# A two-layer relational graph convolution: a third pass of summing tiles from x, and the order of its steps

## The chip, the cores and the metric

The kernel runs on one core of one Trainium2 chip. The core has five engines that run side by side and meet at semaphores: PE (TensorE, matrix products into PSUM), DVE (VectorE), ACT (ScalarE), POOL (GpSimd) and SP (SyncE). Here POOL issues the indirect gathers, and SP and ACT issue all other DMAs. The metric is the time of one execution on the device in microseconds (us), as the median of several runs.

## The reference

There are 12500 nodes with 128 features each and 200000 edges, sorted by destination, each with one of eight types. A layer takes, for each node and each type, the mean over the node's edges of this type of the source's features times the type's matrix, adds up the types, adds the node's own features times a root matrix and a bias, and ends with a relu and a residual:

```python
W = jnp.einsum('rb,bio->rio', comp, basis)
xw = jnp.einsum('ni,rio->nro', x, W)
msgs = xw[src, et]
seg = dst * N_REL + et
summed = jax.ops.segment_sum(msgs, seg, num_segments=N_NODES * N_REL)
cnt = jax.ops.segment_sum(jnp.ones((msgs.shape[0],), x.dtype), seg, num_segments=N_NODES * N_REL)
mean = summed / jnp.maximum(cnt, 1.0)[:, None]
agg = mean.reshape(N_NODES, N_REL, HIDDEN).sum(axis=1)
return agg + x @ root + bias
...
for l in range(N_LAYERS):
    h_new = _rgcn_conv(h, src, dst, edge_type, basis[l], comp[l], root[l], bias[l])
    h_new = jax.nn.relu(h_new)
    h = h_new + h
...
x = _layernorm(x + _L0_gnn_ref(x, edge_index, edge_type_8, ...), axis=-1)
```

Only the sources are in no order, so each edge's source row has to be fetched from memory.

## The kernel before

**Tiles and octets.** The edges are cut into 1563 tiles of 128 edges, and eight tiles make an octet; there are 196 octets (the last one is short). Both layers go through the octets in order. In code and text, layer 1 is `l == 0` and layer 2 is `l == 1`. Layer 1 gathers rows of x, takes means by type and only then multiplies by the types' matrices. For layer 2 the finished features are multiplied by all eight matrices ahead of time, into a table `y_d` in memory with one row for each node and type, and layer 2 gathers rows of that table.

**Where a tile's rows come from.** Nearly all tiles get theirs from one indirect DMA each, issued by POOL (`gather`, line 814), into a ring of seven octet buffers (`rows_r`). The gather of octet o + 5 is issued in octet o, into the buffer that octet o - 2 used, so that it waits for PE's means of octet o - 2. The last six octets of a layer are gathered two octets ahead, and behind PE's latest means. 56 tiles of layer 1 are read row by row from SP's and ACT's queues (`lone_rows`, line 750). Eight more, two groups of four (`JOINED`, tiles 1112 to 1115 and 1504 to 1507), are not gathered but *summed from x*.

**Summing four tiles from x** (`joining`). A pass runs through all of x in 98 blocks of nodes. For each block DVE makes a one-hot matrix of 512 edges against the nodes (line 1516), and PE multiplies the block of x with it and adds the product up in the PSUM bank `ct` (line 1531). After 98 blocks each of the 512 edges' columns has its source row; DVE copies the sum out, PE transposes it in four parts, and DVE copies the rows into the buffer `joined`, where PE's means find them as they would find gathered rows. x comes in 13 loads of up to 512 KB over ACT's queue into two buffers (`xb`), and the one-hots have four buffers (`eqb`). `JOINED` gives for each pass its first tile, its first octet and its last: 84 to 132 and 135 to 183, that is two blocks in an octet. `join(o, 0)` issues the loads of octet o, `join(o, 1)` DVE's part, and `join(o, 2)` PE's products for the one-hots made in octet o - 1. The buffers lie in the arena where the destinations and types of the edges stood, so that the checks that read these have to be done before.

**The order in an octet of layer 1** (the loop `for o in range(NG - 3)`). Each engine runs its own instructions in this order: the gather (POOL); the means, 8 products of gathered rows with one-hots of edges (PE, line 1340); `batch`: copies of table halves, of the product before and of the means out of PSUM (ACT); `join(o, 0)`; the single rows; edge preparation; the one-hots for the means of octet o + 2 (DVE, line 1240); `join(o, 1)`; some steps of the checks (`run(later, ...)`); the finishing of nodes; the product of octet o - 1 with the matrices (PE, line 1372); `join(o, 2)`; the placing of octet o - 2 (PE, line 1403); and one or two halves of the table's tiles from octet 50 on (PE, line 1558, with a copy by ACT or DVE), two as long as more than six wait and in the last 16 octets. The class `Plan` turns this one list into waits: an instruction waits for the writer and the readers of what it touches that stand *ahead of it in the list*.

**The checks.** A generator (`checks`) gives 124 steps: the second layer's matrices, 13 times 7 steps on edges, 11 on spans, 9 on places, 11 of a fix list for the first 16 tiles of layer 2 (`fix_list`, PE lines 1167 and 1188), and a last one. It starts in octet 43, when the edges are prepared, with three steps an octet up to octet 83 and one from 84 on.

**The turn of the layers.** The first two octets of layer 2 are gathered from the part of the table that belongs to the first 94 node tiles; octet 2 begins with one gather of the fix list (line 808) and waits for the whole table.

Of the kernel before, what the change touches and what calls it, by code (L numbers as in the profile page):

```python
# [428 lines left out]
def ordered_path(  # L429
# [26 lines left out]
    P = 128  # L456
# [11 lines left out]
    Q = 8  # L468
# [20 lines left out]
    SOON = 16  # L489
    DONE = NT - 4  # L490
    LONG = 9
    JOINED = [(1112, 84, 132), (1504, 135, 183)]
    SUMMED = {52: (3, 45), 98: (49, 91), 144: (95, 137), 190: (141, 183)}
    assert D == P and R * K == P and B == BF + 1 and 1 < TL and LAST < P and BF % 4 == 0 and Q == G and N % 2 == 0
    main = slice(HALO, HALO + P)
# [5 lines left out]
    def keep(shape, dtype, name):  # L501
        return const.tile(shape, dtype, name=name)
# [71 lines left out]
    def part_of(n, *cell):  # L574
        nonlocal free_at
        free_at += n
        assert free_at <= at
        used_c.append(cell)
        return arena[:, free_at - n:free_at], cell

    M = 4
    xb_b = [part_of(S * D, "xb", i) for i in range(2)]
    eqb_b = [part_of(M * P, "eqb", i) for i in range(4)]
    ends_b = part_of(M * P, "ends")
    joined_b = [part_of(M * P, "joined", i) for i in range(len(JOINED))]
    joined = {t + i: (joined_b[k][0][:, i * P:(i + 1) * P], [joined_b[k][1]])
              for k, (t, _, _) in enumerate(JOINED) for i in range(M)}
    room_c += used_c
    p_8 = keep([P, S + 2], F32, "p_8")
# [2 lines left out]
    first = keep([P, B], F32, "first")  # L592
# [53 lines left out]
    def vec(emit, reads=(), writes=()):  # L646
        plan.add("DVE", emit, reads, writes)
# [4 lines left out]
    def pe(emit, reads=(), writes=()):  # L652
        plan.add("PE", emit, reads, writes)
# [4 lines left out]
    def load(out_t, in_t, reads=(), writes=(), q="SP"):  # L658
        e = nc.sync if q == "SP" else nc.scalar
        plan.add(q, lambda: e.dma_start(out_t, in_t), reads, writes, lane="hw" if q == "SP" else "aq")  # L660
# [7 lines left out]
    def in_turn(emits):  # L668
        def emit():
            for e in emits:  # L670
                last = e()
            return last

        return emit
# [592 lines left out]
    def shape_of(n):  # L1267
        m = min(GN, N - n * GN)
        return (P, S) if m == GN else (m // 2, 2)

    def in_rows(a, n):
        p, k = shape_of(n)
        return a[n * GN:n * GN + p * k, :].rearrange("(p s) d -> p (s d)", s=k)
# [201 lines left out]
    def joining(k):  # L1475

        tile0, first, end = JOINED[k]
        n = end - first + 1
        slots = [(g, i) for g in range(NX) for i in range(shape_of(g)[1])]
        assert len(slots) == NT  # L1480
        takes = {q: [] for q in range(first - 1, end + 3)}
        for j in range(NT):
            takes[first + j * n // NT].append(j)
        used = {g: [q for q, js in takes.items() if any(slots[j][0] == g for j in js)] for g in range(NX)}
        loads = {}
        for g in range(NX):
            loads.setdefault(max(first - 4 + g, JOINED[k - 1][2] + 2 if k else 0) if g < 2 else used[g - 2][-1] + 2, []).append(g)
        (e_t, e_c), (f_t, f_c), (j_t, j_c) = ends_b, eqb_b[0], joined_b[k]
        f3, j3 = (t.rearrange("p (t c) -> p t c", t=M) for t in (f_t, j_t))
        b, bc = ct_b  # L1490
        done = end + 1
        assert max(len(v) for v in takes.values()) <= 2
        assert tile0 // Q >= done + 3 and (k == 0 or first >= JOINED[k - 1][2] + 3)

        def load_b(g):
            p, m = shape_of(g)
            t, c = xb_b[g % 2]
            load(t[:p, :m * D], in_rows(x, g), [], [c] + (free_c if k == 0 and g < 2 else []), "ACT")

        def start_of(q):  # L1500
            if q == first - 4:
                assert checked and parts is None
                load(j_t.bitcast(I32), bass.AP(tensor=src.tensor, offset=src.offset + tile0 * P,
                                               ap=[[0, P], [1, M * P]]), [], [j_c] + free_c, "ACT")
            for g in loads.get(q, ()):
                load_b(g)

        def before(q):
            if q == first - 2 and k == 0:
                x_nodes()  # L1510
            if q == first:
                vec(lambda: nc.vector.tensor_copy(e_t, j_t.bitcast(I32)), [j_c], [e_c] + (free_c if k == 0 else []))
            for j in takes.get(q, ()):
                p = shape_of(slots[j][0])[0]
                o, oc = eqb_b[j % 4]
                vec(lambda j=j, p=p, o=o: nc.vector.tensor_tensor(  # L1516
                    o[:p], e_t[:p], x_node[:p, j:j + 1].to_broadcast([p, M * P]), op=ALU.is_equal),
                    [e_c, "x_node"], [oc])
            if q == done + 1:
                vec(lambda: nc.vector.tensor_copy(f3, b), [bc], [f_c])  # L1520
            if q == done + 2:
                vec(lambda: nc.vector.tensor_copy(j3, b), [bc], [j_c])
            plan.mark("DVE")

        def after(q):
            for j in takes.get(q - 1, ()):
                g, i = slots[j]
                p, m = shape_of(g)
                t, c = xb_b[g % 2]
                o, oc = eqb_b[j % 4]  # L1530
                pe(lambda j=j, p=p, i=i, t=t, o=o: nc.tensor.matmul(  # L1531
                    b.rearrange("p t c -> p (t c)"), t[:p, i * D:(i + 1) * D], o[:p], start=j == 0, stop=j == NT - 1),
                    [c, oc], [bc])
            if q == done + 1:
                pe(in_turn([lambda i=i: nc.tensor.transpose(b[:, i, :], f3[:, i, :], ident) for i in range(M)]),
                   [f_c, "ident"], [bc])
            plan.mark("PE")

        return start_of, before, after

    joins = [joining(k) for k in range(len(JOINED))]

    def join(o, part):
        for (_, first, end), f in zip(JOINED, joins):
            if first - 4 <= o <= end + 3:
                f[part](o)
# [307 lines left out]
    def sup(q):  # L1854
        return (q * Q + G) // (2 * G) - 1
# [13 lines left out]
    def run(gen, n):  # L1869
        for _ in range(n):  # L1870
            if next(gen, gen) is gen:
                return True
        return False
# [39 lines left out]
    def checks():  # L1913
        weights(1, (pt_b, pt_b))
        yield
        for b in range(B):
            yield from check_edges(b)
        yield from check_span()
        yield from check_place()
        yield from fix_list()  # L1920
        yield check_all()

    later = checks()
# [32 lines left out]
    for o in range(NG - 3):  # L1956
        if o + CLOSE == NQ - 2:
            gather(0, NQ - 1)
        gathers(0, o)
        means(o)  # L1960
        batch(o)
        join(o, 0)
        if o == 1:
            where()
            load_offsets()
        if o > 1:
            lone_rows(0, "SP", o)
        for i in range(2 if o < FIRST else 1):
            if parts is not None and run(parts, 1):
                parts = None  # L1970
        onehot(0, o + 2, o - 1)
        join(o, 1)
        if parts is None:
            run(later, 3 if o < 84 else 1)
        if o > 1:
            lone_rows(0, "ACT", o)
        if not opened:
            end()
        for step in opened:
            step()  # L1980
        opened.clear()
        if o > 0:
            product(o - 1)
            if o < SOLO:
                take_product(o - 1)
            else:
                late_y.append(o - 1)
        for step in behind:
            pe(*step)
            plan.mark("PE")  # L1990
        behind.clear()
        join(o, 2)
        if o > 1:
            k = place(o - 2)
            close(k)
            if k is not None and k % S == S // 2 and k // S + 1 < NX:
                n = k // S + 1
                turned_to.extend([turn_x(n, h) for h in range(-(-shape_of(n)[1] // 4))])
                turned_to.append((lambda n=n: load_x(n + 1), None))
        for i in range(2):  # L2000
            if turned_to:
                a, b = turned_to.pop(0)
            elif tables and o >= TABLE and (i == 0 or len(tables) > 6 or o > NG - 16):
                a, b = tables.pop(0)
            else:
                break
            while copies:
                copies.pop(0)(vcopy)
            a()
            if b is not None:  # L2010
                copies.append(b)
# [69 lines left out]
    for q in range(NQ):  # L2081
# [4 lines left out]
        k = sup(q)  # L2086
# [116 lines left out]
```

## Time and profile before

| | |
|---|---|
| median of 3 runs | 3730.01 us (3728.68 to 3738.03) |
| the profiled execution | 3738.43 us |
| its span, first to last instruction | 3736.6 us |
| PE busy | 2986.0 us (80%) |
| DVE busy | 2354.0 us (63%) |
| ACT busy | 354.5 us (9%) |
| POOL busy | 2812.0 us (75%) |
| DMA, mean | 80 GB/s |
| granted PE clock, mean | 0.937 |

Times in the profile are microseconds from the first instruction. A row of a group reads: line, engine, operation, what it writes from what it reads, shapes, count, then busy time in us and the mean of one in ns, then the idle time of the engine just before these instructions and what ended most of it. "issue" is idle time that ends with nothing that the profile shows. A row of a timeline reads: start, length, engine, line, operation, operands, count, and in brackets the idle time before and what ended it. A row by stretches reads: stretch, its length, then busy time and count for each engine shown (PE, its weight loads, DVE, ACT, POOL in this order, or one engine alone), the granted PE clock, the share of the DMA engines' time, and GB/s.

### The profile page before, as it was taken

The numbers are of one execution on the slowest core, as the hardware profiler recorded it, in microseconds if no ns is written. First come the engines' busy times: TensorE is split into PE (matmuls) and PEld (weight loads), VectorE is DVE, ScalarE is ACT, GpSimd is POOL, SyncE is SP. The second block draws the span as 40 slices with busy tenths as digits, with TensorE's granted clock in tenths as the row PEclk, the third lists the DMA queues.
The fourth block names the chain that finished last, engine by engine and source line by source line (L and its number), as shares of the span: only waits on it lengthen the run. The fifth ranks groups of instructions, "written<-read, shape, count | busy, mean of one in ns | idle before, by whom it ended". The sixth has DMA issues, their size and how long they took to land.

```text
span 3736.6 us, 69352 instructions
## 1 busy us (share of the span) xinstructions
PE 2986.0 (80%) x13831; PEld 2137.2 (57%) x13831; DVE 2354.0 (63%) x5786; ACT 354.5 (9%) x795; POOL 2812.0 (75%) x2977
## 2 busy tenths in 40 slices
PE   5777757778877778877778888888888888798896
PEld 3666645565655556655555555555555555555554
DVE  5556435545554445445456778787777787787885
ACT  1121212111111111111100000000000000000000
POOL 7777777777777777777777777777777777777776
PEclk7999889989999999999989999999999999999998
DMA  4122123334333333332332222222222222222222
GB/s 126 55 62 61 56 89 106 117 115 123 112 101 100 91 104 106 95 106 92 99 97 56 55 56 67 67 62 67 56 73 62 62 67 62 67 66 56 68 66 61
DMA packets 159970, 299.91 MB, mean 80 GB/s; under 512 B 67108, under 2 KB 90358, under 8 KB 159534
## 3 DMA queue, kind: packets, MB, share of 16 engines
q0 software_dynamic: 95008, 194.77, 20.4%
q10 hardware_dynamic: 34755, 68.94, 5.7%
q1 hardware_dynamic: 29771, 31.73, 3.2%
q14 instruction: 325, 2.66, 0.2%
q8 instruction: 111, 1.82, 0.2%
HBM read 236.52 MB, written 58.65 MB: 79 GB/s over the span
## 4 chain that ended last, share of the span: by engine, by line
POOL 47%; issue 17%; PE 16%; DMA 9%; ACTq 4%; ACT 3%; DVE 2%; SPq 1%; POOLq 0%; DVEq 0%
POOL rows L814 47%; DMA rows<-y_d,idy 7%; PE y L1372 4%; ACTq L750 3%; PE s L1340 3%; PE s L1726 2%; PE pt L1558 1%; ACTq L745 1%; PE ct L1531 1%; ACT sT L663 1%; SPq L750 1%; ACT y_row L663 1%; DVE dm L1240 1%; PE ct L1010 1%; PE ct L1011 1%
## 5 line engine op out<-in xcount | busy, mean ns | idle before, releaser
L814 POOL DMA_INDIRECT rows<-in_x_dram,idx x1499 | 1420.0, 947 | 459.8 <-issue 451.1
L814 POOL DMA_INDIRECT rows<-y_d,idy x1469 | 1390.0, 946 | 449.8 <-issue 440.2
L1726 PE MATMUL s<-dm,rows 128*128 128x256 f32 x2932 | 777.2, 417 | 260.7 <-DMA rows<-y_d,idy 235.8
L1240 DVE TENSOR_SCALAR dm<-cols,near,w 128x256 f32<-128x256 f16 x1531 | 709.6, 537 | 386.1 <-PE s L1726 376.4
L1726 PEld LDWEIGHTS s<-dm,rows 128*128 128x128 f32 x2932 | 592.4, 210 | 376.4 <-DMA rows<-y_d,idy 233.7
L1240 DVE TENSOR_SCALAR dm<-cols,kr,w 128x128 f32<-128x128 f16 x1563 | 525.9, 403 | 137.4 <-PE s L1340 112.5
L1372 PE MATMUL y<-w_sb,sT 128*128 128x128 f32 x3136 | 443.8, 300 | 203.9 <-ACT ys L663 150.6
L1372 PEld LDWEIGHTS y<-w_sb,sT 128*128 128x128 f32 x3136 | 406.7, 209 | 240.3 <-ACT ys L663 177.6
L1340 PEld LDWEIGHTS s<-dm,rows 128*128 128x128 f32 x2998 | 382.2, 201 | 184.0 <-issue 159.1
L1340 PE MATMUL s<-dm,rows 128*128 128x128 f32 x2998 | 401.6, 287 | 100.5 <-DMA rows<-in_x_dram,idx 90.4
L1619 DVE TENSOR_TENSOR arena<-arena,cols 128x1024 f32<-128x1024 int32 x264 | 319.9, 1212 | 0.0
L1628 PE MATMUL pt<-arena,idx 128*128 128x512 f32 x528 | 269.6, 592 | 0.0
L1628 PE MATMUL y<-arena,idx 128*128 128x512 f32 x528 | 269.6, 592 | 0.0
L1558 PE MATMUL pt<-w_sb,arena 128*128 128x512 f32 (+1 forms) x386 | 206.3, 616 | 63.0 <-DVE y_row L666 43.9
L666 DVE COPY y_row<-pt 128x512 f32<-128x512 f32 x56 | 38.7, 692 | 309.9 <-PE pt L1558 309.9
L663 ACT ACTIVATE sT<-s 128x512 f32<-128x512 f32 x391 | 213.4, 605 | 87.0 <-PE s L1340 86.7
L1516 DVE TENSOR_TENSOR arena<-arena,cols 128x512 f32<-128x512 f32 (+1 forms) x196 | 125.7, 683 | 115.0 <-PE ct L1531 112.2
L1531 PE MATMUL ct<-arena 128*128 128x512 f32 x392 | 187.1, 600 | 0.0
L663 ACT ACTIVATE y_row<-pt 128x512 f32<-128x512 f32 (+1 forms) x139 | 83.0, 597 | 1044.1 <-PE s L1340 846.8
L1628 PEld LDWEIGHTS y<-arena,idx 128*128 128x128 f32 x528 | 100.3, 190 | 126.3 <-issue 126.3
L1619 DVE TENSOR_TENSOR y_row<-arena,cols 128x1024 f32<-128x1024 int32 x128 | 155.1, 1212 | 0.0
L1834 ACT ACTIVATE st<-st,eps 128x8 f32<-128x8 f32 x12 | 3.7, 310 | 1543.8 <-DMA sT<-y_d 1302.3
(253 smaller groups left out, 2300.0 us busy)
## 6 DMA issues: line engine op xcount, KB each, us to landing
sT<-y_d SPq DMA_DIRECT2D x3968, 0.5 KB
sT<-y_d ACTq DMA_DIRECT2D x3968, 0.5 KB
y_d<-y_row ACTq DMA_DIRECT2D x96, 512.0 KB
mixer<-in_x_dram ACTq DMA_DIRECT2D x2304, 0.5 KB
rows<-in_x_dram,idx POOLq DMA_INDIRECT x1499
rows<-y_d,idy POOLq DMA_INDIRECT x1469
jmp<-in_x_dram SPq DMA_DIRECT2D x1408, 0.5 KB
comp_sb<-in_x_dram SPq DMA_DIRECT2D x1408, 0.5 KB
```

The costliest lines, as they stand in the source:

```text
L663: act(lambda: nc.scalar.activation(out_t, in_t, AF.Copy), reads, writes)
L750: return [eng.dma_start(o[j * ch + i:j * ch + i + 1, :].bitcast(byte), table_b[bass.ds(v, 4 * D)].rearrange("(p d) -> p d", p=1)) for i, v ...
L814: ins.append(nc.gpsimd.indirect_dma_start(out=t[:, i - q * Q, :], out_offset=None, in_=table_t, in_offset=bass.IndirectOffsetOnAxis(ap=ids ...
L1240: emits.append(lambda i=i: nc.vector.tensor_scalar(t[:, i - q * Q, :wide], cols[:, :wide], ids[:, i:i + 1], w[:, i:i + 1], op0=ALU.is_equa ...
L1340: last = nc.tensor.matmul(s_b[i // 4][0][:, i % 4, :], lones[i][0] if i in lones else t[:, i, :], d[:, i, :], start=True, stop=True)
L1372: last = nc.tensor.matmul(y[:m], t[:, r, :nt, :].rearrange("p t k -> p (t k)"), w_sb[:, 0, r, :], start=(r == 0), stop=(r == R - 1))
L1516: vec(lambda j=j, p=p, o=o: nc.vector.tensor_tensor(o[:p], e_t[:p], x_node[:p, j:j + 1].to_broadcast([p, M * P]), op=ALU.is_equal), [e_c, ...
L1531: pe(lambda j=j, p=p, i=i, t=t, o=o: nc.tensor.matmul(b.rearrange("p t c -> p (t c)"), t[:p, i * D:(i + 1) * D], o[:p], start=j == 0, stop ...
L1558: pe(lambda: nc.tensor.matmul(hb[:n].rearrange("p r d -> p (r d)"), hT[:, j * P:j * P + n], w_sb[:, 1, k * H:(k + 1) * H, :].rearrange("p ...
L1619: vec(lambda j=j, e=e: nc.vector.tensor_tensor(e, edge, node_p[:, j:j + 1].to_broadcast([P, Q * P]), op=ALU.is_equal), [edge_c, "node"], h ...
L1628: pe(lambda j=j, m=m, o=o, e=e, h=h, b=b: nc.tensor.matmul(b.rearrange("p t c -> p (t c)"), o[:m], e[:m, 4 * h * P:4 * h * P + 4 * P], sta ...
L1726: ins = nc.tensor.matmul(a, lones[i][0] if i in lones else t[:, i, :], d[:, i, :], start=(opens and i == 0), stop=(last and i == n - 1 and ...
```

## The change

Six edits belong together:

- `JOINED` has three passes for two: tiles 888 to 891 in octets 70 to 106, tiles 1200 to 1203 in 109 to 145, and tiles 1515 to 1518 in 148 to 184. Each pass has 37 octets instead of 49, so two or three blocks in an octet. Twelve tiles of layer 1 are summed from x where eight were.
- The buffer of the joined rows stays double; the third pass uses the first one again.
- `join(o, 2)` stands right behind `join(o, 0)`: PE's block products come after the octet's means and ahead of the product of octet o - 1, and in the list ahead of `join(o, 1)`, DVE's one-hots of the same octet.
- The transposes of a finished pass are moved on by one octet with it (`done + 2` for `done + 1`).
- The checks take five steps an octet up to octet 63, and one from 64 on.
- The assertions follow: up to three blocks an octet, and no new sources in a buffer whose tiles are still to be used.

```diff
-    JOINED = [(1112, 84, 132), (1504, 135, 183)]
+    JOINED = [(888, 70, 106), (1200, 109, 145), (1515, 148, 184)]
...
-    joined_b = [part_of(M * P, "joined", i) for i in range(len(JOINED))]
-    joined = {t + i: (joined_b[k][0][:, i * P:(i + 1) * P], [joined_b[k][1]])
+    joined_b = [part_of(M * P, "joined", i) for i in range(2)]
+    joined = {t + i: (joined_b[k % 2][0][:, i * P:(i + 1) * P], [joined_b[k % 2][1]])
...
-        (e_t, e_c), (f_t, f_c), (j_t, j_c) = ends_b, eqb_b[0], joined_b[k]
+        (e_t, e_c), (f_t, f_c), (j_t, j_c) = ends_b, eqb_b[0], joined_b[k % 2]
...
-        assert max(len(v) for v in takes.values()) <= 2
+        assert max(len(v) for v in takes.values()) <= 3
+        assert k < 2 or first - 4 > JOINED[k - 2][0] // Q
...
-            if q == done + 1:
+            if q == done + 2:
                 pe(in_turn([lambda i=i: nc.tensor.transpose(b[:, i, :], f3[:, i, :], ident) for i in range(M)]),
                    [f_c, "ident"], [bc])
...
         join(o, 0)
+        join(o, 2)
         if o == 1:
             where()
             load_offsets()
...
-            run(later, 3 if o < 84 else 1)
+            run(later, 5 if o < 64 else 1)
...
         behind.clear()
-        join(o, 2)
         if o > 1:
```

## The prediction

> **What bounds the kernel now.** I read the page first (groups and chain), then all instructions of the gather's line, then POOL against time, then PE and DVE in the octets that the change touches.
>
> ```profile
> span 3736.6 us, 69352 instructions
> ...
> POOL 47%; issue 17%; PE 16%; DMA 9%; ACTq 4%; ACT 3%; DVE 2%; SPq 1%; POOLq 0%; DVEq 0%
> ...
> L814 POOL DMA_INDIRECT rows<-in_x_dram,idx x1499 | 1420.0, 947 | 459.8 <-issue 451.1
> L814 POOL DMA_INDIRECT rows<-y_d,idy x1469 | 1390.0, 946 | 449.8 <-issue 440.2
> ```
>
> The chain is led by the gathers (line 814) and by "issue", time in which an engine waits for nothing that is shown. Busy 75% does not sound like a bound, so the question is what the other 25% of POOL is. All instructions of line 814, and what ended POOL's idle time before them:
>
> ```profile
> L814 POOL DMA_INDIRECT rows<-in_x_dram,idx x1499: 943/947/1248, 4.5 to 1881.1; - x188
> L814 POOL DMA_INDIRECT rows<-y_d,idy x1469: 943/947/1038, 1882.4 to 3722.9; - x184
> ...
>   issue: 891.4, 2918
>   DMA rows<-y_d,idy: 4.6, 15
>   PE s L1726: 3.8, 9
>   PE ct L1531: 2.7, 9
> ```
>
> 891.4 us over 2918 gaps is 0.305 us each, and the gaps put down to others are as long (4.6/15, 2.7/9): a fixed step between two gathers, no wait. Where the chain leaves POOL through such a gap it goes over to PE without need. From 4.5 to 3722.9 us lie 2969 gathers (one more, line 808, between the layers), 2968 steps of 1.253 us. Before the first is 4.5 us, behind the last 3736.6 - 3722.9 - 0.9 = 12.8. So the span is a count of gathers times 1.253 us. POOL against time, in its order around the turn from layer 1 to layer 2:
>
> ```profile
> 1881.14 0.94 POOL L814 DMA_INDIRECT rows<-in_x_dram,idx  x1 [0.30 <-issue]
> 1882.39 0.95 POOL L814 DMA_INDIRECT rows<-y_d,idy  x1 [0.30 <-issue]
> ...
> 1901.15 0.95 POOL L814 DMA_INDIRECT rows<-y_d,idy  x1 [0.30 <-issue]
> 1903.19 0.94 POOL L808 DMA_INDIRECT jmp<-y_d,fix_i  x1 [1.10 <-DMA y_d<-y_row]
> ```
>
> Even the turn costs only 1.10 - 0.30 = 0.8 us, in front of octet 2 of layer 2, which waits for the last store of the table.
>
> **What goes.** Tiles 888-891, 1200-1203 and 1515-1518 are no longer gathered; 1112-1115 and 1504-1507 are again. That is 1495 gathers for 1499: -4 x 1.253 = **-5.0 us**, on the path, if POOL stays unblocked and nothing lengthens a gather.
>
> **What comes: a third pass.** A pass is 98 one-hots on DVE and 98 block products on PE; two of them are in the page:
>
> ```profile
> L1516 DVE TENSOR_TENSOR arena<-arena,cols 128x512 f32<-128x512 f32 (+1 forms) x196 | 125.7, 683 | 115.0 <-PE ct L1531 112.2
> ...
> L1531 PE MATMUL ct<-arena 128*128 128x512 f32 x392 | 187.1, 600 | 0.0
> ```
>
> One more adds 98 x 0.683 = 67 us to DVE (less where they overlap) and 187.1/2 = 94 us to PE, 0.95 us for each product, and on ACT's queue 13 loads of x and one of the sources, beside DVE, PE and ACT work of at most a few us for turning the sums. None of this is POOL's. It costs nothing while POOL runs free: gather of octet q+7 takes the buffer of octet q (a ring of 7) and so waits for that octet's means. The cover is thus the gathers that POOL may still issue when PE comes to octet q. POOL's gathers from the start up to four moments at which PE began the means of octets 8, 70, 84 and 112:
>
> ```profile
> 0.00:136.30 136.30, 99.88 (x105) 0.81 0.35 104
> ...
> 0.00:697.20 697.20, 524.05 (x553) 0.90 0.28 82
> 0.00:842.06 842.06, 633.78 (x668) 0.90 0.29 88
> 0.00:1099.40 1099.40, 828.16 (x874) 0.92 0.31 93
> ```
>
> By the lists in the code, the gathers through octet 8 are 72, through octet 70 549, 84 657, 112 872. So PE was 33 gathers behind at octet 8, 4 at 70, 11 at 84 and 2 at 112; two are the landing of the rows. POOL stalls when it has issued all through octet q+6, which is some 47 gathers, 59 us, behind. Even 33 blocked nothing.
>
> **PE's octet in the passes.** PE where it was behind, with two blocks an octet, and the start of two octets without blocks:
>
> ```profile
> 811.62 1.95 PE L1340 MATMUL s<-dm,rows 128*128 128x128 f32 x16
> ...
> 819.73 1.95 PE L1340 MATMUL s<-dm,rows 128*128 128x128 f32 x16
> ...
> 870.28 1.95 PE L1340 MATMUL s<-dm,rows 128*128 128x128 f32 x16
> 873.09 2.05 PE L1372 MATMUL y<-w_sb,sT 128*128 128x128 f32 x16 [0.85 <-ACT ys L663]
> 874.97 1.88 PE L1531 MATMUL ct<-arena 128*128 128x512 f32 x4
> 876.69 0.59 PE L1403 MATMUL po<-pl,ys 128*128 128x256 f32 x2
> ...
> 877.35 1.02 PE L1558 MATMUL pt<-w_sb,arena 128*128 128x512 f32 x2
> 879.15 1.13 PE L1558 MATMUL pt<-w_sb,arena 128*128 128x512 f32 x2 [0.79 <-DVE y_row L666]
> 880.12 1.95 PE L1340 MATMUL s<-dm,rows 128*128 128x128 f32 x16
> ```
>
> 8.1 us without blocks, 9.8 with two; POOL's octet is 1499/195.4 = 7.67 gathers x 1.253 = 9.6. 98 blocks in 37 octets are 2.65 for 2.0: +0.65 x 0.95 = +0.6 us. The block sums now stand between the means and the product, so the product's wait of 0.85 us for ACT, which evacuates the product before, lies under at least 1.7 us of them: -0.85. An octet with two table halves thus takes 9.8 + 0.6 - 0.85 = 9.6 us, POOL's own pace, and one with a single half (from about octet 97, when the tables' backlog is worked off) some 1.8 less. PE neither falls behind for long nor catches up at once.
>
> **The moved block sums, one by one.** What stands behind them on PE is the product, the placing and the tables, up to 2.8 us later than the means; ACT's evacuation of the means starts as before. The octet's one-hots come from DVE an octet earlier, so PE finds them ready. DVE loses room: with three a time and four buffers, its one-hots of octet o wait for PE's sums in that same octet, where until now the sums of the octet before were enough. It ran about two octets ahead, stopped by PE:
>
> ```profile
> 1256.66 2.64 DVE L1240 TENSOR_SCALAR dm<-cols,kr,w 128x128 f32<-128x128 f16 x8 [3.05 <-PE s L1340]
> 1259.22 0.48 DVE L1253 TENSOR_SCALAR pl<-cols,pos 128x256 f32<-128x256 f16 x1
> 1261.29 1.29 DVE L1516 TENSOR_TENSOR arena<-arena,cols 128x512 f32<-128x512 f32 x2 [1.59 <-PE ct L1531]
> ```
>
> Behind that wait stand the finishing adds, the table copies and the one-hots of means three octets on; PE's next block sums wait for it. PE's block sums end some 4.5 us into its octet, two one-hots take 1.4, so they are ready 5.9 us in, and PE asks for them 9.6 + 2 in: 5.7 us to spare. Cost 0, between -0.85 per octet (if more is hidden) and +1.4 (if the two one-hots show in full).
>
> **The checks.** POOL and DVE in two stretches, and the fix list on PE:
>
> ```profile
> 500.00:600.00 100.00, 62.57 (x356) 47.97 (x355) 38.96 (x123) 15.22 (x35) 75.74 (x80) 0.86 0.35 112
> ...
> 2000.00:2200.00 200.00, 167.44 (x578) 108.98 (x579) 145.85 (x308) 1.59 (x2) 151.12 (x161) 0.96 0.26 56
> ```
>
> ```profile
> 797.88 6.66 PE L1167 MATMUL pt<-arena 128*128 128x16 f32 x32 [1.82 <-ACT sT L663]
> ...
> 823.65 1.95 PE L1188 MATMUL pt<-arena 128*128 128x3 f32 x16 [1.97 <-ACT ys L663]
> ...
> 834.96 1.95 PE L1188 MATMUL pt<-arena 128*128 128x3 f32 x16 [0.85 <-ACT ys L663]
> ```
>
> Of the 124 steps, 105 are done in octets 43 to 63, five at a time; the rest follow one an octet, to octet 82 instead of 84. A step works on a quarter of what a block's one-hot (0.683 us) works on; two more are estimated at no more than 0.7 us, in an octet of a DVE that is busy 39% there (first row, third engine); cost 0. The fix list's steps fall in octets 71 to 81, inside pass 1, instead of 80 to 83 ahead of it, and PE is kept by them for 8.5 + 3.9 + 2.8 = 15 us: 12 gathers. With the 4 of octet 70 that is 16 behind, with some drift perhaps 20, of 47. Cost 0.
>
> **The loads.** ACT's first load overwrites what the checks read; those are done in octet 63 and the load is issued in 66. Each 512 KB of x is asked for two octets (19 us) ahead rather than three, and PE never waited for one (line 1531 has no such wait). On ACT a few issues stand in front of the single-row reads; cost 0.
>
> **The turn of the layers.** The last gather of layer 1 ends at 1882.08, the last table store lands at 1903.19: 21.1 us, against 16 gathers, 20.0. This store moves with the gathers as long as PE works on their heels, and it does:
>
> ```profile
> 1860.00 3.54 PE L1340 MATMUL s<-dm,rows 128*128 128x128 f32 x16 [4.46 <-DMA rows<-in_x_dram,idx]
> ```
>
> The third pass ends on PE in octet 187, before that. The stall of 0.8 us stays.
>
> **Sum.** The profiled execution took 3738.43 (span 3736.6); -5.0 gives 3733.4 and a span of 3731.6. It is 8.4 us (0.2%) above the median of the runs shown, 3730.01; by the same difference the median becomes **3725.0 us**, ratio 0.9987. Measurement of this kernel can tell about 0.3%, 11.2 us, from no change; this lies within it.
>
> **Rivals.** (a) PE starves POOL. If the handshake costs PE, one octet after another, the 1.4 us above and the 0.85 is not won, its octet is 9.8 + 0.6 + 1.4 = 11.8, it loses 2.2 us on POOL in each of the 27 octets 70 to 96: 59 us, on top of 16 gathers (20 us), of 59. POOL then stands still for 20 us: 3725 + 20 = 3745. It decides from 39/27 = 1.4 us lost per octet on. For it: PE and DVE would be tied in each octet. Against: 5.7 us to spare. (b) The turn does not move: the tail of layer 1 is 43 us of PE, ACT and stores behind the row at 1860.00. If that row were not set by the gathers, octet 2 would wait 5 us longer: 3730. Against it: PE waited 4.46 us for rows there. (c) DVE and POOL get in each other's way. If each added one-hot held a gather for its whole length, +67 us: 3792. Against it: POOL is busy 75.7% of 500 to 600 us, with DVE at 39%, and 151.12/200 = 75.6% of 2000 to 2200, with DVE at 73%. (d) More than 0.3% is won; no stall is there to be removed but the 0.8 us.
>
> On (c) the Trainium skill, "SBUF — State Buffer", section "Who interferes with whom", says that VectorE and GpSimd share a port pair under an exclusive lock, and that a VectorE instruction with at most one SBUF input outside the two-port modes stays out of it. The one-hot reads one operand from the bank of columns in PSUM, so by that rule too nothing is added; the trace agrees, with gathers of 943 to 947 ns beside one-hots.
>
> **Chances.** Forecast 0.80, (a) 0.09, (b) 0.07, (c) 0.02, (d) 0.02. Within 0.3%: forecast, (b), and none of the others, 0.87. Slower 0.11; faster 0.02. Range 3721 to 3736: below, -5.8 with the turn's stall gone and three us of spread of runs; above, (b) and half the 8 us by which the slowest run shown lies over the median, or a short stall of kind (a). The likeliest alone: 3722 to 3728.
>
> **What would show it.** 1495 gathers from in_x_dram, each 947 ns with 0.305 us before it; the first from y_d at about 1877.4; the last at about 3717.9; 588 records of line 1531; the product's wait for ACT gone in octets 70 to 184; PE fewer than 30 gathers behind at octet 97. Wrong if a gather waits tens of us for PE s or ct, if the table's store holds octet 2 by 5 us, or if the step between gathers is not 1.253.

## The result and the profile after

| | before | after |
|---|---|---|
| median of 22 runs each | 3730.28 us (3728.67 to 3738.03) | 3725.41 us (3723.83 to 3727.22) |
| the profiled execution | 3738.43 us | 3725.31 us |
| its span | 3736.6 us | 3723.5 us |
| PE busy | 2986.0 us | 3046.8 us |
| DVE busy | 2354.0 us | 2412.4 us |
| POOL busy | 2812.0 us | 2801.2 us |

The ratio is 0.9986, with a 95% interval of 0.998 to 0.9992: 4.9 us less, 0.13% (3.0 to 7.5 us by that interval). The forecast was 3725.0 us and no change that can be told.

The page of the kernel after, its span, its chain and its largest groups (line numbers behind the changed block are one higher than before):

```profile
span 3723.5 us, 69868 instructions
...
POOL 48%; issue 17%; PE 15%; DMA 11%; DVE 3%; ACTq 3%; ACT 1%; SPq 1%; POOLq 0%; DVEq 0%
...
L814 POOL DMA_INDIRECT rows<-in_x_dram,idx x1495 | 1412.8, 945 | 458.3 <-issue 449.9
L814 POOL DMA_INDIRECT rows<-y_d,idy x1469 | 1386.4, 944 | 449.3 <-issue 435.8
```

The bound is the same: the gathers, and the "issue" between them. Four gathers fewer stand in the first row. All instructions of line 814 of the kernel after (shortest, median and longest in ns, first and last start in us), and what ended POOL's idle time before them:

```profile
L814 POOL DMA_INDIRECT rows<-in_x_dram,idx x1495: 940/944/1331, 4.5 to 1872.4; - x187
L814 POOL DMA_INDIRECT rows<-y_d,idy x1469: 940/944/1046, 1873.6 to 3709.8; - x184
...
  issue: 885.7, 2901
  DMA rows<-y_d,idy: 7.7, 25
  PE s L1727: 4.3, 12
  PE ct L1532: 2.1, 7
```

No gather waits for the third pass: the seven gaps put down to the block products (line 1532) are 2.1/7 = 0.3 us long, which is the gap that every gather has. What the third pass added, from the page's groups of the kernel after:

```profile
L1517 DVE TENSOR_TENSOR arena<-arena,cols 128x512 f32<-128x512 f32 (+1 forms) x294 | 193.9, 680 | 373.3 <-PE ct L1532 373.2
...
L1532 PE MATMUL ct<-arena 128*128 128x512 f32 (+1 forms) x588 | 278.3, 606 | 0.0
```

That is 193.9 - 125.7 = 68 us more on DVE and 278.3 - 187.1 = 91 us more on PE, for 5 us less on POOL. DVE's one-hots now wait 373 us in all for PE's sums, against 112 before, and PE's sums never waited (the 0.0 at the end of the second row).

The two profiled executions differ by 13.1 us, not by 4.9. The profiled one of before was as slow as the slowest of its runs. The step between two gathers was (3709.8 - 4.5)/2964 = 1.2501 us after, and 1.2528 us before; 2964 steps of 0.0027 us are 8.1 us, and four gathers 5.0. Of the 8.1 us, 7.0 lie in the gathers' own length: by the busy times and counts of their groups it is 946.8 ns before and 944.4 ns after. Another 0.7 us lie in two stalls that were shorter: the one at the turn of the layers, and one gather near the end of layer 2 that waited for PE (1.33 us at 3690.39 before, 0.91 us at 3677.35 after).

The 2.4 ns are not the work of the change. In the fourteen traces of this case the median gather takes 947 ns in five and 944 ns in nine, and nothing lies between. It goes neither by the kernel (the same kernel with four passes, `e4_four_passes` and `e6_four_passes_again`, has 944 and 947) nor by the chip (of the first four experiments below, on one chip, `e1_skip12` has 947 and the others 944). So the profiled execution of before was one of the slower kind. An estimate from the median of before, less the 1.8 us between time and span, the 4.5 us ahead of the first gather and the 13.7 us from the last one's start on, gives a step of 3710.3/2968 = 1.2501 us, the same as after.

### The profile page after: what moved, and what is told of

Same layout as the page of the kernel before. It is cut to its first block, busy times and chain, and to the rows that moved or that the text cites. A ratio compares the mean times of both kernels' runs of the same rounds, so it can differ in the third digit from the quotient of the medians.

```text
span 3723.5 us, 69868 instructions
## 1 busy us (share of the span) xinstructions
PE 3046.8 (82%) x14031; PEld 2159.1 (58%) x14031; DVE 2412.4 (65%) x5887; ACT 354.6 (10%) x795; POOL 2801.2 (75%) x2973
## 4 chain that ended last, share of the span: by engine, by line
POOL 48%; issue 17%; PE 15%; DMA 11%; DVE 3%; ACTq 3%; ACT 1%; SPq 1%; POOLq 0%; DVEq 0%
POOL rows L814 48%; DMA rows<-y_d,idy 9%; PE s L1340 3%; PE y L1372 3%; ACTq L750 2%; PE s L1727 2%; PE ct L1532 2%; PE pt L1559 2%; DVE dm L1240 1%; SPq L750 1%; DMA rows<-in_x_dram,idx 1%; ACTq L745 1%; ACT sT L663 1%; PE ct L1010 1%; PE po L1403 1%
## 5 line engine op out<-in xcount | busy, mean ns | idle before, releaser
L1727 PEld LDWEIGHTS s<-dm,rows 128*128 128x128 f32 x2932 | 595.6, 211 | 377.4 <-DMA rows<-y_d,idy 229.0
L1340 PE MATMUL s<-dm,rows 128*128 128x128 f32 x2990 | 417.3, 295 | 146.9 <-DMA rows<-in_x_dram,idx 131.7
L1340 PEld LDWEIGHTS s<-dm,rows 128*128 128x128 f32 x2990 | 394.7, 208 | 235.7 <-issue 211.1
L1372 PEld LDWEIGHTS y<-w_sb,sT 128*128 128x128 f32 x3136 | 392.7, 200 | 165.1 <-ACT sT L663 71.6
L1372 PE MATMUL y<-w_sb,sT 128*128 128x128 f32 x3136 | 410.6, 287 | 94.2 <-ACT sT L663 52.6
L1517 DVE TENSOR_TENSOR arena<-arena,cols 128x512 f32<-128x512 f32 (+1 forms) x294 | 193.9, 680 | 373.3 <-PE ct L1532 373.2
L1532 PE MATMUL ct<-arena 128*128 128x512 f32 (+1 forms) x588 | 278.3, 606 | 0.0
L1532 PEld LDWEIGHTS ct<-arena 128*128 128x128 f32 (+1 forms) x588 | 107.5, 199 | 91.2 <-issue 91.2
```

Of the source, the lines that this page charges most:

```text
L1340: last = nc.tensor.matmul(s_b[i // 4][0][:, i % 4, :], lones[i][0] if i in lones else t[:, i, :], d[:, i, :], start=True, stop=True)
L1372: last = nc.tensor.matmul(y[:m], t[:, r, :nt, :].rearrange("p t k -> p (t k)"), w_sb[:, 0, r, :], start=(r == 0), stop=(r == R - 1))
L1517: vec(lambda j=j, p=p, o=o: nc.vector.tensor_tensor(o[:p], e_t[:p], x_node[:p, j:j + 1].to_broadcast([p, M * P]), op=ALU.is_equal), [e_c, ...
L1532: pe(lambda j=j, p=p, i=i, t=t, o=o: nc.tensor.matmul(b.rearrange("p t c -> p (t c)"), t[:p, i * D:(i + 1) * D], o[:p], start=j == 0, stop ...
L1727: ins = nc.tensor.matmul(a, lones[i][0] if i in lones else t[:, i, :], d[:, i, :], start=(opens and i == 0), stop=(last and i == n - 1 and ...
```

## The experiments

**The theory** was that the span is a count of gathers, so that four fewer are worth 5 us, that the moved products and the third pass cost nothing, and that a fourth pass would be worth as much again. **The rivals**: that POOL is not the bound, so that the count is worth nothing; and that the move itself or the changed checks, not the count, carried the difference.

### The count, the move, two and four passes

`e1_skip12` leaves twelve more gathers out of the kernel after; these tiles get rows of other tiles.

```diff
               for k, (t, _, _) in enumerate(JOINED) for i in range(M)}
+    joined.update({t + i: joined[JOINED[k][0] + i] for k, t in enumerate((896, 1208, 1504)) for i in range(M)})
```

> Twelve more tiles of layer 1 (896-899, 1208-1211, 1504-1507) are neither gathered nor summed: their means read the rows of the joined tiles, so that this part of the result is left out. No work is added. If the time is the number of gathers times 1.25 us, 12 gathers fewer than in the changed kernel take 15.0 us: 3710.4 us, with 0.30 us still in front of nearly every gather and the first gather of layer 2 15 us earlier. If the turn of the layers is set by PE's tail and not by the gathers, octet 2 of layer 2 waits for the table longer than 0.8 us and less than 15 us is won. If PE is the bound in layer 1, nothing is won: 3725.

`e2_move_alone` is the kernel before with the moved products alone.

```diff
-            if q == done + 1:
+            if q == done + 2:
...
         join(o, 0)
+        join(o, 2)
...
-        join(o, 2)
         if o > 1:
```

> The kernel before with one edit: the blocks' products stand behind the means and in front of the product. Two passes, 1499 gathers. If the gathers set the time, it is that of before, 3730.3 us within 1 us, while the product's wait for ACT's copy of the product before (150.6 us, 137 times) goes from the octets with blocks, about 100 of them, and falls to about 50 us, and PE waits longer for gathered rows (90 us before, more than 130). If the order matters for the time, it is 1 us or more off 3730.3.

`e3_two_passes` is the kernel after without its third pass, so with the count of before.

```diff
-    JOINED = [(888, 70, 106), (1200, 109, 145), (1515, 148, 184)]
+    JOINED = [(888, 70, 106), (1200, 109, 145)]
```

> The changed kernel without its third pass: the new order, the new checks, passes of 37 octets for tiles 888-891 and 1200-1203; tiles 1515-1518 are gathered. 1499 gathers as before. If the number of gathers is all, 3730.4 us, that is before's time, although two thirds of the change stand. If the denser passes or the earlier checks bring or cost anything of their own, it differs from before by that. If the third pass cost something, it would be less than 5 us slower than the changed kernel.

`e4_four_passes` has a fourth pass, in 27 octets each, and up to four blocks an octet.

```diff
-    JOINED = [(888, 70, 106), (1200, 109, 145), (1515, 148, 184)]
+    JOINED = [(816, 70, 96), (1040, 99, 125), (1280, 128, 154), (1504, 157, 183)]
...
-        assert max(len(v) for v in takes.values()) <= 3
+        assert max(len(v) for v in takes.values()) <= 4
```

> The changed kernel with four passes of 27 octets (tiles 816-819 in octets 70-96, 1040-1043 in 99-125, 1280-1283 in 128-154, 1504-1507 in 157-183), three or four blocks an octet: 1491 gathers. If only POOL's count matters as long as PE is fewer than about 47 gathers behind: another 5.0 us off the changed kernel, 3720.4. PE's octet with two table halves is 9.03 us in the changed kernel (octets 84 to 96) and would be 0.98 x 0.87 = 0.85 us longer, 9.9, against 9.6 of POOL: it falls some 7 us further behind to octet 97, far from 59. If the handshake of DVE and PE over four one-hot buffers costs PE time once all four are in use in each octet, PE falls behind by more than 1.4 us an octet, gathers wait for PE, and the time is above 3725.

Measured, beside a kernel before of 5686.83 us (5667.26 to 5713.27) on that chip:

| kernel | median | range | ratio to before, 95% |
|---|---|---|---|
| e1_skip12 | 5703.05 us | 5681.69 to 5726.23 | 1.0028 [1.0008, 1.0048] |
| e2_move_alone | 5701.42 us | 5684.06 to 5720.60 | 1.0023 [1.0004, 1.0042] |
| e3_two_passes | 5694.76 us | 5652.70 to 5714.14 | 1.0003 [0.998, 1.0025] |
| e4_four_passes | 5706.43 us | 5682.83 to 5714.73 | 1.0016 [0.9997, 1.0034] |

All four expectations missed: every kernel, the one before too, takes 5.7 ms on this chip and not 3.73. The page of `e3_two_passes`, chain and first group:

```profile
SPq 51%; issue 32%; PE 5%; another core or an unknown queue 5%; ACTq 3%; DVE 2%; ACT 1%; DMA 1%; DVEq 0%
...
L814 POOL DMA_INDIRECT rows<-in_x_dram,idx x1499 | 1415.1, 944 | 1373.7 <-PE s L1340 747.8
```

POOL is not in the chain any more. Its gathers take 944 ns as ever, but their idle time is three times as long, and more than half of it is now spent waiting for PE's means, which free the ring. At the head stands SP's queue, with the row by row reads. All instructions of line 750 of `e3_two_passes` on that queue in layer 2 (shortest, median, longest in ns):

```profile
L750 SPq MOVE sT<-y_d x3968: 2/29/1410, 2841.9 to 5672.7; - x199
L750 SPq DMA_DIRECT2D sT<-y_d x3968: 2/228/1409, 2842.0 to 5672.7; - x199
```

The same of the kernel after, on the chip of its profile:

```profile
L750 SPq MOVE sT<-y_d x3968: 29/29/29, 1895.5 to 3637.4; - x199
L750 SPq DMA_DIRECT2D sT<-y_d x3968: 224/228/623, 1895.6 to 3637.5; - x199
```

The medians agree; but a register move that takes 29 ns in each of 3968 cases there takes up to 1410 ns here. So on this chip single instructions of the queues were held up, and SP's list became the bound. The sizes fit: in the trace of `e3_two_passes` 935 of SP's 8194 register moves take 0.65 to 0.80 us, and 1987 gaps between its instructions are as long, where the trace of the kernel after has no such move and one such gap. At about 0.7 us each (an estimate) that is 2.0 ms, about what the kernel takes longer. What held them up stays open. This was nobody's theory, but it is a control: where POOL is not the bound, sixteen gathers fewer than before (`e1_skip12`) gain nothing. By how much `e1_skip12` and `e2_move_alone` are slower than before, 0.2 to 0.3%, says nothing of a kernel that POOL bounds.

### Two and four passes on another chip

The same two kernels, on another chip, to see whether the four gathers show there.

> The changed kernel without its third pass, once more, on a chip on which the single-row reads are not what bounds it (the run before, on another chip, took 5694.8 us beside 5686.8 of the kernel before, with SP's row reads at the head of the chain). 1499 gathers as before. If the number of gathers is all, the time of before, 3730.3 us within 1 us. If the order, the denser passes or the earlier checks bring or cost anything of their own, it differs from before by that. If the third pass cost something of its own, this would be less than 5 us slower than the changed kernel's 3725.4.

> The changed kernel with four passes of 27 octets, three or four blocks an octet, once more on another chip: 1491 gathers. If only POOL's count matters as long as PE is fewer than about 47 gathers behind: another 5.0 us off the changed kernel's 3725.4, that is 3720.4. PE's octet with two table halves would be 9.03 + 0.98 x 0.87 = 9.9 us against POOL's 9.6: some 7 us further behind at octet 97 than the changed kernel. If the handshake of DVE and PE over four one-hot buffers costs PE more than 1.4 us an octet, gathers wait for PE, and the time is above 3725.

The kernel before took 5684.70 us (5671.31 to 5715.60). `e5_two_passes_again` took 5693.51 us (5679.06 to 5742.23), ratio 1.0009 [0.9988, 1.0031]; `e6_four_passes_again` took 5701.75 us (5680.24 to 5719.05), ratio 1.0019 [1.0001, 1.0036]. The chip was like the first, the expectations missed in the same way, and nothing new is learned on the change.

### Without the row by row reads

If SP's and ACT's lists are the bound there, a kernel that gathers those tiles too should be faster there, and show the count again. In both kernels the lists were emptied, so that the 56 tiles of layer 1 and those of layer 2 are gathered:

```diff
-        [("SP", 91, 1552, 45, 32, 15, ...
+        [("SP", 91, 91, 45, 32, 15, ...
...
-            load_offsets()
```

> The kernel before without the single-row reads on SP's and ACT's queues: those 56 tiles of layer 1 and 62 of layer 2 are gathered by POOL like the others (1555 + 1531 gathers, and the one of the fix list). On the chips of the runs so far the row reads led the chain and the time was 5.69 ms, so that POOL's count could not show. If the gathers set the time once the row reads are gone, it is 3087 steps of 1.25 us and 17 us beside them: 3876 us, nearly 1.8 ms less than the kernel before on the same chip although POOL has 118 gathers more. If something else is slow on these chips (PE, ACT), it stays well above 4000 us.

> The changed kernel, also without the single-row reads: 1551 + 1531 gathers, and the one of the fix list; all three passes, the moved products and the earlier checks as in the changed kernel. Against the same edit of the kernel before (run beside it): 5.0 us less if four gathers are what the change is worth, with 0.3 us still in front of nearly every gather. No difference if the turn of the layers or PE takes it up; 15 us or more above it if PE, with a third pass, starves POOL.

The kernel before took 5681.85 us there. `e7_all_gathered_before` took 4673.02 us (4662.32 to 4690.60), `e8_all_gathered_after` 4682.80 us (4673.29 to 4692.56). Without the lists the kernel is 1.0 ms faster on such a chip: they were what bound it. But POOL is still not. The page of `e7_all_gathered_before`:

```profile
another core or an unknown queue 37%; PE 27%; DVE 26%; issue 6%; ACT 4%; DMA 0%; ACTq 0%; DVEq 0%
...
L814 POOL DMA_INDIRECT rows<-in_x_dram,idx x1555 | 1473.2, 947 | 917.0 <-issue 423.3
```

and of `e8_all_gathered_after`:

```profile
L814 POOL DMA_INDIRECT rows<-in_x_dram,idx x1551 | 1468.8, 947 | 930.6 <-issue 423.1
```

The chain runs over PE and DVE, and 37% of it is put down to "another core or an unknown queue", which the undisturbed chip's chains do not have: instructions of PE, DVE, ACT and POOL were held up too, and by what stays open. Of 917 us of POOL's idle time only 423 are the fixed gaps. The medians, 0.21% apart in the other direction, lie in overlapping ranges. So this chip can't price a gather in this way either.

### POOL made the bound by itself

To have POOL as the bound with room for all others, 32 small fills were put on POOL behind each octet's gathers, up to octet 189 of both layers: in the kernel before, the kernel after, and the latter with two and with four passes. Each of these is the kernel named, with its passes as above, and

```diff
+    fill = keep([P, 48], I32, "fill")
...
+        if q < NQ - LATE:
+            for _ in range(32):
+                pool(lambda: nc.gpsimd.iota(fill, pattern=[[1, 48]], base=0, channel_multiplier=0), [], ["fill"])
```

> The kernel before with POOL's octet made longer by a fixed piece: behind each octet's gathers, up to octet 189, POOL fills a small scratch tile 32 times, each fill behind the one before. On the chips of these runs the other engines take some 12 to 14.5 us for an octet, so that POOL's 9.6 us do not set the time; with some 10 us more (32 fills of about 0.3 us, an estimate from the index fills at the start, 0.12 to 0.34 us each) POOL's octet is near 20 us and should be the bound again. If so, POOL's busy time and its fixed gaps fill the span, and the time is about 2 x 190 x 10 + 3730 = 7.5 ms (the fills' own length decides it, and nothing hangs on it).

> The changed kernel with the same fills. The fills are the same number, so that only the gathers differ: 1495 for 1499 in layer 1. If the change is worth its four gathers wherever POOL is the bound: 5.0 us less than the kernel before with fills. If the turn of the layers or the third pass takes it up: no difference or more. If DVE's added one-hots lengthen gathers, the mean gather in this trace is longer than beside it.

> The changed kernel without its third pass, with the same fills: the moved products, the denser passes and the earlier checks stand, and the gathers are 1499 as before. If only the count of gathers matters: the time of the kernel before with fills, within 1 us, and 5.0 us more than the changed kernel with fills. If the order brings or costs time of its own where POOL is the bound, it differs from the kernel before with fills by that.

> The changed kernel with four passes of 27 octets and the same fills: 1491 gathers. If the price is 1.25 us for each gather: 10.0 us less than the kernel before with fills, 5.0 less than the changed kernel with fills. If three or four blocks an octet cost PE or DVE time that POOL has to wait for, less than that is won, and gathers stand behind PE s or PE ct for more than the fixed 0.3 us.

The chip was undisturbed: the kernel before took 3731.15 us (3729.18 to 3732.23) on it, without fills. With fills:

| kernel | gathers, layer 1 | median | range | to e9_long_before |
|---|---|---|---|---|
| e9_long_before | 1499 | 6648.56 us | 6647.31 to 6649.66 | |
| e10_long_after | 1495 | 6644.57 us | 6643.81 to 6645.21 | -3.99 us |
| e11_long_two | 1499 | 6648.52 us | 6648.15 to 6648.73 | -0.04 us |
| e12_long_four | 1491 | 6640.84 us | 6640.63 to 6641.10 | -7.72 us |

The fills were shorter than expected, so the level of 7.5 ms is a miss. The groups of POOL in `e9_long_before`:

```profile
L839 POOL IOTA fill<- 128x48 int32 x12064 | 2032.3, 168 | 800.2
L815 POOL DMA_INDIRECT rows<-in_x_dram,idx x1499 | 1416.5, 945 | 502.9 <-issue 496.8 <-DMA arena<-in_dst_dram 2.3 <-PE pt L943 1.1
```

A fill takes 0.168 us and 0.066 us of gap before it (800.2/12064). The gathers still come with fixed gaps (0.54 us where a fill stands ahead, 0.30 us elsewhere), and nearly none waits for anything. The same group of `e10_long_after`, then of `e11_long_two` and `e12_long_four`:

```profile
L815 POOL DMA_INDIRECT rows<-in_x_dram,idx x1495 | 1412.9, 945 | 503.4 <-issue 481.7 <-PE ct L1536 17.4 <-DMA arena<-in_dst_dram 2.4
```

```profile
L815 POOL DMA_INDIRECT rows<-in_x_dram,idx x1499 | 1415.6, 944 | 504.5 <-issue 489.1 <-PE ct L1536 8.2 <-DMA arena<-in_dst_dram 2.4
```

```profile
L815 POOL DMA_INDIRECT rows<-in_x_dram,idx x1491 | 1408.1, 944 | 505.2 <-issue 491.9 <-PE ct L1536 6.6 <-DMA arena<-in_dst_dram 2.3
```

What follows: where POOL is the bound, the time goes with the number of gathers, over 0, 4 and 8 gathers left out, and the ranges of the three do not overlap. Two passes with the moved products and the changed checks give what the kernel before gives, to 0.04 us: these edits neither gain nor cost, as long as POOL leaves PE room. This throws out the second rival for a kernel that POOL bounds with room to spare. That POOL is the bound without fills too is read from the profiles before and after, in which all but two of its gaps are the fixed ones; it speaks against the first rival. A gather taken out is worth 1.00 us (3.99/4) and 0.97 us (7.72/8) here, and not the 1.25 us of its step. One part of the difference can be seen: the busy time falls by 3.6 us for four gathers (1416.5 - 1412.9; four of 0.945 us are 3.8), but the idle time before the remaining gathers rises by 0.5 us, where it should fall by four gaps. In `e10_long_after` there is one gap that is 1.58 us longer than the usual 0.30; POOL against time:

```profile
2140.03 0.94 POOL L815 DMA_INDIRECT rows<-in_x_dram,idx  x1 [0.54 <-PE ct L1536]
2142.86 0.94 POOL L815 DMA_INDIRECT rows<-in_x_dram,idx  x1 [1.88 <-issue]
2144.10 0.94 POOL L815 DMA_INDIRECT rows<-in_x_dram,idx  x1 [0.31 <-issue]
```

`e11_long_two` has one such gap and `e12_long_four` two (1.90 us each); `e9_long_before` has none above 1.1 us. Nothing that the profile shows ends them. The profiled spans of `e9_long_before` and `e10_long_after`, 6646.7 and 6643.3 us, differ by 3.4 us, that is 5.0 less 1.6. But this one gap is not shown to be the reason: `e11_long_two` has it too and takes no longer than `e9_long_before`, its gathers being 0.3 ns shorter, 1.0 us in all. Nor are the 0.97 us of `e12_long_four` all price: up to the start of the last gather (6633.0 and 6626.6 us) the profiled executions differ by 6.4 us, 0.80 for each gather, and the other 1.3 us lie behind it, where 12.4 us are left for 13.7. So a gather's price is measured here to some 0.2 us and no better. What makes the gaps, and whether they are there in each run that is not profiled, stays open.

**Not tried.** With the fills PE has 17.4 us for an octet (the fills start from 14.4 to 6592.6 us, over 377 octets) where it has 9.6 without them, so `e12_long_four` does not show that four passes are hidden in the kernel without fills. On an undisturbed chip that was not measured, nor were the move alone and the two passes without fills; there the price of the four gathers rests on the medians before and after alone. Nor was it tried how much more work PE can take in the passes before POOL stalls, or a third pass without the move.

## Why the prediction was right, point by point

**The bound.** Right. 2969 less 4 gathers, each with its fixed gap, make up the span after as before. One reading was too smooth: of the nine gaps put down to PE s (line 1726) before, one was 1.33 us long and not 0.3, so there were two stalls, the turn's 0.8 us and this one's 1.0, and both fell (to 0.5 and 0.6). The control on the disturbed chips shows the other side, that the count is worth nothing where a queue of SP is the bound.

**-5.0 us for four gathers.** The medians differ by 4.87 us. With fills the same four are worth 3.99 us. Both lie inside what the forecast's own range allowed. That puts the price at 1.0 to 1.2 us for each gather by the medians, but the interval of the first difference, 3.0 to 7.5 us, allows 0.7 to 1.9; that the median came within 0.4 us of the forecast is in part luck.

**The profiled execution.** This is the term that was mis-sized. The prediction took the step of the profiled execution before, 1.253 us with gathers of 947 ns, as a constant of the kernel; it was 1.250 with gathers of 944 to 945 ns in the profiled execution after. So the span came out 8.1 us below the forecast (3723.5 for 3731.6), the first gather from y_d 3.8 us earlier (1873.6 for 1877.4) and the last 8.1 us earlier (3709.8 for 3717.9). The median came out right because the prediction took the 8.4 us between the profiled execution and the median off again, without knowing that they belonged to that one execution: after the change the profiled execution lies 0.1 us from the median.

**The product's wait for ACT.** Right: gone. PE's waits for the product from line 1372 between 855 and 1790 us of the kernel before (us in total, times, longest):

```profile
PE y L1372 <- ACT ys L663: 104.9, 98, 2.6
```

The same of the kernel after, between the same marks, and its first row:

```profile
PE s L1340 <- DMA rows<-in_x_dram,idx: 103.0, 54, 4.2
...
PE y L1372 <- ACT ys L663: 6.0, 9, 1.2
```

The time PE won went into a wait for rows: it was on POOL's heels more often (54 times for 36), which costs nothing.

**PE's octet of 9.6 us.** Too long, on the safe side. PE against time in two octets of the first pass of the kernel after, one with three blocks and one with two:

```profile
866.59 1.95 PE L1340 MATMUL s<-dm,rows 128*128 128x128 f32 x16
868.37 2.74 PE L1532 MATMUL ct<-arena 128*128 128x512 f32 x6
870.95 1.95 PE L1372 MATMUL y<-w_sb,sT 128*128 128x128 f32 x16
...
875.20 1.13 PE L1559 MATMUL pt<-w_sb,arena 128*128 128x512 f32 x2 [0.78 <-DVE y_row L666]
876.16 1.95 PE L1340 MATMUL s<-dm,rows 128*128 128x128 f32 x16
877.95 1.88 PE L1532 MATMUL ct<-arena 128*128 128x512 f32 x4
...
884.65 1.95 PE L1340 MATMUL s<-dm,rows 128*128 128x128 f32 x16
```

9.57 us and 8.49 us. The first has one more small product (line 1405); the second has none, as the octet of before from 880.12 to 889.73 us, with two blocks too, which took 9.61. So the wait of 0.85 us is gone, and another 0.3 us that the prediction didn't have. POOL's octet is 9.6, so PE gained on POOL all through the pass.

**The cover.** Right, with more to spare than said. POOL's gathers up to the moments at which PE began the means of octets 8, 73, 84 and 97 of the kernel after (count in brackets):

```profile
0.00:136.60 136.60, 100.04 (x106) 0.81 0.37 103
0.00:737.00 737.00, 554.14 (x585) 0.90 0.30 85
0.00:839.20 839.20, 631.41 (x667) 0.91 0.32 90
0.00:956.30 956.30, 719.84 (x761) 0.93 0.33 95
```

By the lists the gathers through these octets are 72, 572, 657 and 757. PE was 34, 13, 10 and 4 gathers behind, where the prediction had 16 to 20 for the passes and POOL stalls at some 47.

**The fix list, 15 us.** Too high in its place. Its first part fell into octet 72:

```profile
724.84 5.25 PE L1167 MATMUL pt<-arena 128*128 128x16 f32 x32 [1.40 <-DVE arena L1162]
```

It took 5.25 + 1.40 us for the 6.66 + 1.82 of before; the later part, 32 records of line 1188 for both kernels, was spread over octets. Hidden, as forecast.

**The handshake, 0.** Right. DVE's one-hots do wait for PE's sums of their own octet, 373 us in all for 112; PE's next sums found them ready each time (idle 0.0). Rival (a), 3745 us, had DVE and PE tied; it would have needed 1.4 us lost per octet, and PE won some.

**The turn of the layers.** Right: the stall went along with the gathers. POOL against time in the kernel after:

```profile
1872.40 0.94 POOL L814 DMA_INDIRECT rows<-in_x_dram,idx  x1 [0.30 <-issue]
1873.64 0.95 POOL L814 DMA_INDIRECT rows<-y_d,idy  x1 [0.30 <-issue]
...
1892.37 0.94 POOL L814 DMA_INDIRECT rows<-y_d,idy  x1 [0.30 <-issue]
1894.13 0.94 POOL L808 DMA_INDIRECT jmp<-y_d,fix_i  x1 [0.82 <-DMA y_d<-y_row]
```

0.82 - 0.30 = 0.5 us for the 0.8 of before. Rival (b), 5 us of wait there, is out.

**DVE and POOL in each other's way.** Rival (c), 3792 us, is out: 98 one-hots more, and a gather takes no longer: 944 to 945 ns for 946 to 947 in the two profiles, and 944.4 ns in both kernels with fills, with 196 one-hots (`e9_long_before`) and with 294 (`e10_long_after`). The page of the Trainium skill that the prediction named ("SBUF — State Buffer", section "Who interferes with whom") agrees with this. Rival (d), more than 0.3% won, is out as well: 0.13% was.

## What to carry to other kernels

An engine that is busy 75% of the time can be the bound throughout: look at what ends its idle time, and if nearly all of its gaps are alike and put down to "issue", count its instructions and multiply. Then work can be given to engines that are behind in nothing, as long as one counts how far the bound engine may run ahead of them: here 159 us of PE and DVE work paid for 5 us of POOL. A step taken from one profiled execution is good to about 0.2% of the span, which is more than such a change is worth, so a forecast of a median should be a difference set on the median.

## What was not expected of the hardware

- The step between two gathers differs from one execution to the next (1.2528 and 1.2501 us), 8.1 us over the kernel. Most of it is the gather's own length: its median was 947 ns in five traces and 944 ns in nine, with the same kernel and on the same chip in either. What sets it stays open.
- On two chips the queues of SP and ACT held up single instructions for up to 1.4 us that take 0.029 or 0.228 us otherwise. The kernel takes 5.68 to 5.69 ms there instead of 3.73, and 4.67 ms if it gathers all tiles by POOL. The cause stays open.
- A gather taken away under a POOL bound was worth about 1.0 us with fills beside it, not its full step of 1.25 us, and single gaps of 1.9 us appeared that nothing in the profile ends. Whether the one explains the other is not shown.
